# Layer 0's gate sums on TensorE instead of GpSimd and VectorE, in a two-layer graph kernel with a hand-written order

## The chip, the cores and the metric

The kernel runs on one core of one Trainium2 chip. All data are 32-bit floats. The metric is the device time of one execution in microseconds (us), as the median over runs on the chip. The profile shows one execution: TensorE (PE, with its weight loads as PEld), VectorE (DVE), ScalarE (ACT), GpSimd (POOL), SyncE (SP) and the DMA queues.

## The reference

There are 16 batches (graphs) of 1024 nodes with 128 features, and two layers. Layer 0 is a gated graph attention, layer 1 a convolution with four heads; each ends in a residual sum and a layer norm. Cut to what matters:

```python
# layer 0, x: (16, 1024, 128), adj: (16, 1024, 1024) of zeros and ones
h = einsum('bnf,df->bnd', x, Ww) + Wb
e = einsum('bjl,bkl->bjk', einsum('bjd,dl->bjl', h, A), h)
e = e + swapaxes(e, 1, 2)
attention = softmax(where(adj > 0, e, 0.0), axis=1) * adj
h_prime = relu(einsum('bij,bjk->bik', attention, h))
ic = sigmoid(h_prime @ wi_u + x @ wi_x)[..., None]
fc = sigmoid(h_prime @ wf_u + x @ wf_x)[..., None]
oc = sigmoid(h_prime @ wo_u + x @ wo_x)[..., None]
x = layernorm(x + oc * tanh(ic * h_prime + fc * x))

# layer 1, H = 4 heads
h = einsum('bnf,hfd->hbnd', x, conv_w) + conv_b[:, None, None, :]
scores = einsum('hbni,hij,hbmj->hbnm', h, attn_w, h)
hh = relu(einsum('hbnm,hbmd->hbnd', tanh(adj * scores), h))
x = layernorm(x + relu(relu(mean(hh, axis=0)) + x))
```

The change is about the three gates `ic`, `fc`, `oc`, and there about the part `h_prime @ w_u`: per batch 1024 nodes times 128 features against three weight vectors.

## The kernel before

**Batches and layers are interleaved.** Layer 1 of batch b is the backbone: 4 heads of 8 steps, each step two half steps, so 64 half steps a batch. In one step TensorE computes the scores of 128 nodes against all 1024 in two products of 512 columns (`sc`), VectorE multiplies them with the adjacency into `pair`, and ScalarE takes tanh. The pairs of the steps before are multiplied with `h` by a scheme of seven products of 64 x 256 tiles in place of eight (`early`, `late`, in `Pair.product`). It needs sums of rows, which VectorE makes (`differ`, `differ_more`), and one sum that a DMA of GpSimd's queue accumulates.

**Layer 0 of batch b + 1** is strewn over these half steps. Its pieces have letters: W, L, X load; Q and H project; S scores one row block, T turns it over a DRAM transfer; E finds the edges (GpSimd); A takes the row maximum and the exponentials; B weights the row and multiplies it with h (TensorE, G for the second half); R0 and R1 apply relu and leave `hpT`, h_prime with features on partitions (128 x 1024). P turns `hpT` on VectorE and sends it through DRAM to `hp`, with nodes on partitions. Then the gates, I (the inner sum and tanh), O (the outer one), V and N (layer norm), and D, which turns the new x into `x1T` for layer 1.

**The gates before** (batch 1 on). h_prime @ w_u is computed from `hp`: GpSimd multiplies all of `hp` with one broadcast weight vector, `wu_b`, into the buffer of `x1T` (`weigh_hp`, line 620), and VectorE sums over the features (`sum_hp`, lines 626 and 628). This is done three times, once for each gate, one after the other because all three use one buffer: Y multiplies for f, F sums for f and takes its sigmoid, f scales x by that gate on ScalarE and multiplies for i, i sums and multiplies for o, o sums and takes the sigmoid of i and o. The part x @ w_x comes with h's projection: `multiply_h` (line 86 through `mm`) multiplies with 132 columns, of which three are the gates' and are kept in `gate`. Batch 0, whose layer 0 runs ahead of all else, gets its gates from TensorE in `rows_half`, through `ident_g`: the identity with the three u vectors (`gate_u`) beside it.

**The order is written out by hand.** Each engine works in program order, and the program order is in three lists of 64 strings, one string per half step: `FIRST` for batch 0, `PLAN` for the middle ones, `LAST` for batch 15. A plain name is a piece of batch b + 1, `+` marks batch b + 2; `d` and `m` are VectorE's sums for the pairs, `u`, `r` and `j` projections and sums for layer 1, `e` a step of the layer's end. In batch 14 there is no batch 16, so the `+` pieces fall away.

**Products on TensorE.** Once layer 1 has begun, `mm` splits each product into two halves of 64 weight columns, which lie in different column halves of the array. Each half of a 32-bit product appears in the profile as two records, each with a weight load:

```python
for c in range(2):
    nc.tensor.matmul(out[ts(c, HD)], lhsT[:, ts(c, HD)], rhs, start=start, stop=stop)
```

**PSUM.** `small` gives a piece one of three buffers (`ps_sc`), the same that the scores of layer 1 rotate through. A product can start when the engine that reads the buffer's last content is done with it.

Of the kernel before, what the change touches and what calls it, by code (L numbers as in the profile page):

```python
# [11 lines left out]
F32 = mybir.dt.float32  # L12
BF16 = mybir.dt.bfloat16
U8 = mybir.dt.uint8
AF = mybir.ActivationFunctionType
ALU = mybir.AluOpType
AX = mybir.AxisListType
PSUM = bass.MemoryType.PSUM

P = 128  # L20
EPS = 1e-5
# [3 lines left out]
def two_layer_adjacency_kernel(  # L25
# [19 lines left out]
    nc = tc.nc  # L45
    B, N, D = x.shape
    H = conv_w.shape[0]
    assert D == P and N % 512 == 0
    NB = N // P
    NH = N // 512  # L50
    BH = NB // NH

    consts = ctx.enter_context(tc.tile_pool(name="consts", bufs=1))
    adjp = ctx.enter_context(tc.tile_pool(name="adjp", bufs=NB))
    sb = ctx.enter_context(tc.tile_pool(name="sb", bufs=2))
# [7 lines left out]
    def small(name):  # L63

        k = len(made) % (3 + len(spare))
        made.append(name)
        if k < 3:
            return ps_sc.tile([P, 512], F32, tag="sc", name=name)
        n = N if spare[k - 3] == "acc1" else 512
        return ps_acc.tile([P, n], F32, tag=spare[k - 3], name=name)[:, :512]  # L70

# [8 lines left out]
    def mm(out, lhsT, rhs, start, stop):  # L80

        if not begun:
            nc.tensor.matmul(out, lhsT, rhs, start=start, stop=stop)
            return
        for c in range(2):
            nc.tensor.matmul(out[ts(c, HD)], lhsT[:, ts(c, HD)], rhs, start=start, stop=stop)  # L86

    warm = sb.tile([P, N], F32, tag="sum", name="warm", bufs=1)
    nc.vector.memset(warm[:, :P], 0.0)
# [27 lines left out]
    gate_u, gate_x = ident_g[:, D : D + 3], wwT_g[:, D : D + 3]  # L117

    wu_b = consts.tile([P, 3, D], F32, name="wu_b")

    def load_late_weights():
        nc.sync.dma_start(cw_in[0:1], conv_b.rearrange("(o h) d -> o h d", o=1))
        nc.sync.dma_start(cw_last, conv_w[:, D - 1, :].partition_broadcast(P))
        for f0, f1 in ((0, 112), (112, D - 1)):
            nc.sync.dma_start(
                cw_in[1 + f0 : 1 + f1], conv_w[:, f0:f1, :].rearrange("h f d -> f h d")
            )
        nc.sync.dma_start(aw, attn_w.rearrange("h i j -> i h j"))  # L130
        for g, w in enumerate((wi_u, wf_u, wo_u)):
            nc.sync.dma_start(gate_u[:, g : g + 1], w.rearrange("(d o) -> d o", o=1))
            nc.sync.dma_start(wu_b[:, g, :], w.partition_broadcast(P))

# [189 lines left out]
    def turn(dst, src, name):  # L326

        t = sb.tile([P, N], F32, tag="turn", name=f"turn_{name}", bufs=2)
        nc.vector.transpose(t.rearrange("p (k d) -> p k d", d=P), src)
        hop(dst, t, name)  # L330
# [10 lines left out]
    adj_t, x1_t, x1T_t = {}, {}, {}  # L341
# [6 lines left out]
    def layer0(b):  # L348
# [5 lines left out]
        t = {}  # L354
# [257 lines left out]
            hpT = t["hpT"].rearrange("p (k d) -> p k d", d=P)  # L612
            turn(t["hp"], hpT, f"hp_{b}")

        def weigh_hp(g):

            if b not in x1T_t:
                x1T_t[b] = sb.tile([P, N], F32, tag="x1T", name=f"x1T_{b}")
            t["hw"] = x1T_t[b].rearrange("p (k d) -> p k d", d=P)
            nc.gpsimd.tensor_mul(  # L620
                t["hw"], t["hp"], wu_b[:, g : g + 1, :].to_broadcast([P, NB, D])
            )

        def sum_hp(g):
            hw = sb.tile([P, NB, 1], F32, tag="hw", name=f"hws_{b}_{g}")
            nc.vector.tensor_reduce(hw, t["hw"], AX.X, ALU.add)  # L626
            gate = t["gate"][:, :, g : g + 1]
            nc.vector.tensor_add(gate, hw, gate)

        def sigmoid(gate):  # L630

            nc.scalar.activation(gate, gate, AF.Exp, scale=-1.0)
            nc.vector.tensor_scalar_add(gate, gate, 1.0)
            nc.vector.reciprocal(gate, gate)

        def forget():
            t["u"] = sb.tile([P, NB, D], F32, tag="u", name=f"u0_{b}", bufs=1)
            t["x1"] = sb.tile([P, NB, D + 1], F32, tag="x1", name=f"x1_{b}")
            for k in range(NB):
                nc.scalar.mul(t["u"][:, k, :], t["x"][:, k, :], t["gate"][:, k, 1:2])  # L640
            nc.gpsimd.memset(t["x1"][:, :, 0:1], 1.0)

        def gate_f():
            sum_hp(1)
            sigmoid(t["gate"][:, :, 1:2])

        def gate_f_end():
            forget()
            weigh_hp(0)

        def gate_i():
            sum_hp(0)
            weigh_hp(2)

        def gates_io():
            sum_hp(2)
            sigmoid(t["gate"][:, :, 0:3:2])

        def inner(halves):
            u, gate, hp = t["u"], t["gate"], t["hp"]  # L660
# [32 lines left out]
        if b == 0:  # L693
            pieces.update(R2=end_second, q0=copy_q, b0=partial(back, 0))
            for j in (1, 2):
                pieces[f"M{j}"], pieces[f"X{j}"] = partial(mask, j), partial(exponentials, j)
            for q in range(NH):
                for name, piece in (
                    ("R", end_first), ("P", rows_half), ("c", copy_half), ("a", add_gate),
                    ("e", exp_gate), ("d", end_gate), ("f", forget_half),  # L700
                ):
                    pieces[f"{name}{q}"] = partial(piece, q)
                pieces[f"T0.{q}"] = partial(turn_first_score, q)
                pieces[f"S1.{q}"] = partial(score, 1, [q])
        else:
            pieces.update(
                P=turn_hp, Y=partial(weigh_hp, 1), F=gate_f, f=gate_f_end, i=gate_i, o=gates_io,
                R0=partial(end_half, 0), R1=partial(end_half, 1),
            )
            for j in range(NB):  # L710
                pieces[f"G{j}"] = partial(back, j, [1])
            for v in "abcd":
                pieces[f"V{v}"] = lambda: next(t["norm", 0])
# [38 lines left out]
    h1_t, u_t = {}, {}  # L752

    def turn_x1(b):
        turn(x1T_t[b].rearrange("p (k d) -> p k d", d=P), x1_t[b][:, :, 0:D], f"x1_{b}")

    def turn_first_x1(x1, q):
# [309 lines left out]

    ORDER = [m for i in range(BH) for m in (i, i + BH)]
    first, second, join = layer0(0), layer0(1), join_weights()
    run(first, "W L0 L1 L2 L3 L4 L5 L6 L7")  # L1070
    load_late_weights()
# [51 lines left out]
    for g in range(2):  # L1123
# [2 lines left out]


    PLAN = [
        "B3", "E4 L5 T5 m15", "", "j0.0 A4 L6", "", "d0", "E5 T6 m0", "E6 r2 r3 B4",
        "d1 L7 r6 A5 r7", "m1", "B5 j0.1", "A6 d2", "+W E7", "", "u1.0 e", "+Q0 u1.1 m2 B6 A7",  # L1130
        "B7 j1.1 j1.0", "d3", "+L0 m3 e X R0 e", "+E0 G0 G1 G2 e e e G3 G4 G5",
        "G6 G7 e +L1 R1 d4", "P e m4", "", "", "", "+L2", "+E1 d5", "m5 d6 u2.0 e", "+H0 Y +h0",
        "+Q1 m6 F +S0", "+T0", "+H1 u2.1 +A0 +h1 j2.0", "d7 +S1 f i +T1", "", "m7", "o d8 +S2",
        "j2.1", "+S3 u3.0 +T2 m8 I0", "I1", "", "", "d9 O0 +S4", "m9 O1", "Va", "Vb u3.1",
        "+E2 d10", "+S5 m10 Vc", "+T3", "Vd N0 d11 j3.0", "+H2 m11", "+h2 +B0 +L3", "D",
        "d12 +S6", "m12 +T4", "j3.1", "+S7", "d13", "m13 +A1", "", "+E3", "+B1 u0.0",
        "+A2 u0.1 +A3", "+L4", "d14 r5 r0 m14 r4 +B2 d15 r1",
    ]

    FIRST = [  # L1140
        "S5 A0", "m15", "E1 B0", "u1.0", "L3 A1", "S6 d0 E2", "A2 S7 B1 u1.1 m0",
        "L4 B2 T3 T4 L5", "d1 E3", "E4 A3 j1.0 m1", "E5", "T5 B3 d2", "+W A4 L6", "E6", "B4 L7",
        "+Q0 m2 T6 A5", "", "E7 A6 B5 u2.0 d3 u2.1", "+L0 m3 B6 j1.1", "+E0 A7", "+L1 B7 d4",
        "m4", "R0", "", "G0", "+L2 G1 G2", "+E1 G3 G4 d5", "G5 m5 G6 d6 G7", "j2.0 R1 P +H0 +h0",
        "+Q1 m6 +S0 X", "+T0", "+H1 +A0 +h1", "d7 +S1 +T1", "Y", "m7 j2.1", "F d8 +S2", "",
        "+S3 f +T2 m8 i", "", "o", "I0 u3.0 I1", "d9 +S4", "O0 m9 O1", "u3.1", "Va Vb", "+E2 d10",
        "+S5 m10 Vc", "Vd +T3 j3.0", "N0 d11", "+H2 m11", "+h2 +B0 +L3", "D", "d12 +S6",
        "j3.1 m12 +T4", "", "+S7", "d13", "m13 +A1", "", "+E3", "+B1 u0.0", "u0.1 +A2 +A3", "+L4",
        "d14 r0 r5 m14 +B2 d15 r4 r1",
    ]  # L1150

    LAST = [
        "", "m15", "", "j0.0", "", "d0 m0", "", "r7", "r3", "d1", "u1.0 r2 r6 m1", "j0.1 d2", "e",
        "u1.1 j1.1", "m2", "d3", "", "m3", "j1.0", "", "d4", "u2.0 m4", "", "d5", "", "m5 j2.0",
        "", "e", "", "u2.1 d6", "m6", "", "d7", "", "j2.1 m7", "u3.0", "d8", "m8", "", "", "",
        "d9", "m9", "u3.1", "e", "j3.1 d10", "m10", "", "d11 j3.0", "", "m11", "e", "", "e", "e",
        "", "e", "e", "", "e", "", "", "", "",
    ]
    begun.append(True)
    spare.clear()  # L1160
# [2 lines left out]
    for b in range(B):  # L1163
# [37 lines left out]
        for step in range(H * NB):  # L1201
            hd, m = divmod(step, NB)
            i, half = divmod(m, 2)
# [95 lines left out]
```

## Time and profile before

| what | value |
|---|---|
| median of 3 runs | 2328.73 us (2328.29 to 2329.71) |
| the profiled execution | 2329.8 us, its span 2328.0 us |
| layer 1 of batch 0 begins at | 63.4 us |
| one middle batch | 142.5 us |
| batch 15 begins at | 2200.6 us |
| last matmul ends at | 2321.8 us |
| GpSimd's gate products (line 620) | 45, 2.48 us each |
| VectorE's gate sums (line 626) | 45, 1.21 us each |
| gate adds (line 628), scalings (633), reciprocals (634) | 11.5, 8.7, 6.9 us in all |

How to read it: times of rows are sums over the execution, "busy" is the union of an engine's records, and a product's row counts records, four to a product that `mm` splits. The share of an engine is a mean over 16 batches, whose first and last differ from the middle ones; the windows by batch show this. The granted TensorE clock was full but for 3.4 us at half speed, from 163.5 us on.

### The profile page before, as it was taken

How to read it: one execution, taken by the hardware profiler on the slowest of the kernel's cores; microseconds unless marked ns; L12 is line 12 of the kernel's file. 1: busy time of each engine (PE TensorE's matmuls, PEld its weight loads, DVE VectorE, ACT ScalarE, POOL GpSimd, SP SyncE). 2: the span in 40 equal slices, each digit the busy share in tenths (PEclk: the TensorE clock that was granted, in tenths of full speed). 3: DMA queues.
4: the chain of work that ended last, by engine and by line, in shares of the span. 5: the costliest groups of instructions: out<-in, count | busy, mean ns of one | idle time of the engine just before them, and what ended most of it. 6: DMA issues, size and time to landing. Idle time of an engine off the chain costs nothing. (4 is left out here: it accounts for less than half of the span.)

```text
span 2328.0 us, 40444 instructions
## 1 busy us (share of the span) xinstructions
PE 2304.9 (99%) x14693; PEld 1074.7 (46%) x14693; DVE 2039.5 (88%) x3689; ACT 1292.4 (56%) x2186; POOL 1308.2 (56%) x1129
## 2 busy tenths in 40 slices
PE   9999999999999999999999999999999999999998
PEld 5345544444444444444444444444444444444444
DVE  7879898998989889898898988889898898988777
ACT  6545564555556555555555555556556555554444
POOL 2645656556565655656466564665645646555342
PEclk9999999999999999999999999999999999999999
DMA  4647565575655656556565565756647565573421
GB/s 146 164 95 199 124 144 154 114 195 133 170 133 111 190 137 173 132 123 173 134 180 129 129 179 114 184 133 135 171 105 201 130 165 135 106 184 86 123 55 37
DMA packets 498090, 327.27 MB, mean 141 GB/s; under 512 B 391139, under 2 KB 416482, under 8 KB 497891
## 3 DMA queue, kind: packets, MB, share of 16 engines
q1 hardware_dynamic: 459149, 250.68, 38.8%
q0 software_dynamic: 38448, 73.94, 18.1%
q8 instruction: 116, 1.90, 0.3%
q14 instruction: 83, 0.68, 0.1%
q10 hardware_dynamic: 294, 0.07, 0.0%
HBM read 199.04 MB, written 59.51 MB: 111 GB/s over the span
## 5 line engine op out<-in xcount | busy, mean ns | idle before, releaser
L86 PE MATMUL sc<-uT,x1T 128*64 128x512 f32 x4096 | 1054.4, 593 | 4.0 <-ACT uT L283 1.9
L836 ACT ACTIVATE pair<-pair 128x1024 f32<-128x1024 f32 x504 | 533.3, 1058 | 588.9 <-DVE pair L829 278.7
L892 POOL DMA_DIRECT2D pair<-pair x252 | 225.5, 895 | 723.3 <-ACT pair L836 158.2
L831 DVE TENSOR_TENSOR pair<-sc,adj 128x512 f32<-128x512 f32 x504 | 339.1, 682 | 105.1 <-PE sc L86 103.7
L86 PEld LDWEIGHTS sc<-uT,x1T 128*64 128x64 f32 x4096 | 294.1, 137 | 293.8 <-issue 156.8
L829 DVE SCALAR_TENSOR_TENSOR pair<-sc,adj 128x512 f32<-128x512 f32 x504 | 343.0, 684 | 86.0 <-PE sc L86 81.5
L475 POOL TENSOR_SCALAR edge<-ring 128x1024 uint8<-128x1024 f32 x120 | 361.0, 3010 | 25.2 <-DMA ring<-in_adjT_dram 23.4
L840 DVE TENSOR_TENSOR pair<-pair 128x1024 f32<-128x1024 f32 x252 | 328.8, 1305 | 10.6 <-ACT pair L836 10.6
L864 PE MATMUL late<-pair,h 128*64 128x256 f32 x2016 | 304.8, 380 | 3.7 <-DMA pair<-pair 3.6
L864 PE MATMUL early<-pair,h 128*64 128x256 f32 x2016 | 304.1, 379 | 1.3 <-ACT pair L836 1.3
L864 PE MATMUL late<-pair,hx 128*64 128x256 f32 x2016 | 304.1, 380 | 0.0
L864 PEld LDWEIGHTS early<-pair,h 128*64 128x64 f32 x2016 | 145.3, 137 | 289.7 <-issue 255.2
L86 PE MATMUL acc<-R,h 128*64 128x512 f32 x960 | 232.2, 592 | 1.3 <-ACT h L524 1.3
L864 PEld LDWEIGHTS late<-pair,h 128*64 128x64 f32 x2016 | 145.6, 137 | 185.4 <-issue 129.5
L864 PEld LDWEIGHTS late<-pair,hx 128*64 128x64 f32 x2016 | 146.6, 137 | 178.3 <-issue 142.7
L891 DVE TENSOR_TENSOR pair<-pair 128x512 f32<-128x512 f32 x252 | 187.8, 745 | 3.2 <-PE early L864 2.6
L504 ACT ACTIVATE R<-R,nmax 128x1024 f32<-128x1024 f32 x126 | 144.7, 1148 | 62.8 <-DVE nmax L500 56.4
L492 DVE CUSTOM_DVE_ANT_0 R<-R,edge 128x1024 f32<-128x1024 f32 x120 | 172.8, 1440 | 3.3 <-POOL edge L475 3.0
L527 DVE TENSOR_TENSOR R<-R,ring 128x1024 f32<-128x1024 f32 x120 | 161.6, 1347 | 0.0
L864 PE MATMUL early<-pair,hx 128*64 128x256 f32 x1008 | 152.0, 379 | 0.0
L620 POOL TENSOR_TENSOR x1T<-hp,wu_b 128x1024 f32<-128x1024 f32 x45 | 111.7, 2482 | 69.5 <-DVE hws L626 63.3
L936 POOL TENSOR_TENSOR w<-w 128x512 f32<-128x512 f32 x63 | 84.8, 1346 | 96.5 <-DVE w L926 96.3
(214 smaller groups left out, 2831.2 us busy)
## 6 DMA issues: line engine op xcount, KB each, us to landing
adj<-in_adjT_dram SPq DMA_DIRECT2D x128, 512.0 KB, 4.2
pair<-pair POOLq DMA_DIRECT2D x252, 256.0 KB, 3.7
ring<-in_adjT_dram SPq DMA_DIRECT2D x120, 512.0 KB, 5.0
xT<-in_xT_dram SPq DMA_DIRECT2D x16, 512.0 KB, 7.2
x<-in_x_dram SPq DMA_DIRECT2D x16, 512.0 KB, 5.2
dram_hp<-turn_hp SPq DMA_DIRECT2D x15, 512.0 KB, 2.6
hp<-dram_hp SPq DMA_DIRECT2D x60, 128.0 KB, 3.1
dram_x<-turn_x SPq DMA_DIRECT2D x15, 512.0 KB
```

Of the source, the lines that this page charges most:

```text
L86: nc.tensor.matmul(out[ts(c, HD)], lhsT[:, ts(c, HD)], rhs, start=start, stop=stop)
L475: engine.tensor_scalar(m, t["adj", j], 0.0, None, ALU.is_gt)
L492: nc.vector.tensor_tensor_reduce(to[:, ks], s[:, ks], t["edge", j][:, ks], 1.0, nmax, ALU.mult, ALU.max, top)
L504: nc.scalar.activation(row(j), row(j), AF.Exp, bias=t["nmax", j], accum_out=t["z", j])
L527: nc.vector.tensor_mul(s[:, ks], s[:, ks], adj[:, ks])
L829: nc.vector.scalar_tensor_tensor(to, psv, -1.0, adj, op0=ALU.mult, op1=ALU.mult)
L831: nc.vector.tensor_mul(to, psv, adj)
L836: nc.scalar.activation(s, s, AF.Tanh)
L840: nc.vector.tensor_add(t[:, X3 : N12 + 1 : N12 - X3, :], t[:, N12 : N12 + 1, :].to_broadcast([P, 2, 512]), t[:, B22 : B11 + 1, :],)
L864: nc.tensor.matmul(out[ts(q, HD)], w, self.t[:, at, ts(q, HN)], start=(i == 0 and p in (1, 3, 5, 4)), stop=(i == BH - 1), skip_group_check ...
L891: nc.vector.tensor_add(t[:, B22], t[:, B22], t[:, N12])
L892: nc.gpsimd.dma_start(t[:, N21], t[:, B22], accum_op=ALU.add)
```

## The change

From batch 1 on, `h_prime @ w_u` is computed by TensorE from `hpT`, which lies with features on partitions as a product needs it: for each of the 8 blocks of 128 nodes one product with `gate_u` (128 x 3), so the block of `hpT` is the stationary operand and three columns stream. All 24 columns of a batch go into one PSUM tile, `pg`; VectorE adds them to `gate` in one add of 128 x 24, and the sigmoid of all three gates is taken in one chain. `weigh_hp`, `sum_hp`, `wu_b` and its three loads fall away; the x1T buffer is taken when D needs it, no longer for the gates. The piece Y is now the products, the add and the exponential, F the rest of the sigmoid, f the scaling of x; i and o are gone. P and the transfer to `hp` stay, as I needs `hp`.

The three lists are laid out anew. In `PLAN`, R0 moves from half step 18 to 23, R1 from 20 to 27, P from 21 to 28, Y from 28 to 30, F from 29 to 32, f from 32 to 34, I0 from 37 to 35, h0 from 28 to 31, S0 from 29 to 32, T0 from 30 to 33, S3 from 37 to 44 beside S4, and the loads, edges and row pieces of the next batch (L, E, A, B) move by a few half steps each. D stays in 51.

```diff
-    wu_b = consts.tile([P, 3, D], F32, name="wu_b")
...
-            nc.sync.dma_start(wu_b[:, g, :], w.partition_broadcast(P))
...
-        def weigh_hp(g):
-
-            if b not in x1T_t:
-                x1T_t[b] = sb.tile([P, N], F32, tag="x1T", name=f"x1T_{b}")
-            t["hw"] = x1T_t[b].rearrange("p (k d) -> p k d", d=P)
-            nc.gpsimd.tensor_mul(
-                t["hw"], t["hp"], wu_b[:, g : g + 1, :].to_broadcast([P, NB, D])
-            )
-
-        def sum_hp(g):
-            hw = sb.tile([P, NB, 1], F32, tag="hw", name=f"hws_{b}_{g}")
-            nc.vector.tensor_reduce(hw, t["hw"], AX.X, ALU.add)
-            gate = t["gate"][:, :, g : g + 1]
-            nc.vector.tensor_add(gate, hw, gate)
-
-        def sigmoid(gate):
-
+        def gates_T(q):
+
+            if q == 0:
+                t["pg"] = small(f"pg_{b}")[:, : NB * 3]
+            for k in range(q * BH, (q + 1) * BH):
+                mm(
+                    t["pg"][:, ts(k, 3)], t["hpT"][:, ts(k, P)], gate_u,
+                    start=True, stop=True,
+                )
+
+        def gates_in():
+            for q in range(NH):
+                gates_T(q)
+            gate = t["gate"].rearrange("p k g -> p (k g)")
+            nc.vector.tensor_add(gate, t["pg"], gate)
             nc.scalar.activation(gate, gate, AF.Exp, scale=-1.0)
+
+        def gates_end():
+            gate = t["gate"].rearrange("p k g -> p (k g)")
             nc.vector.tensor_scalar_add(gate, gate, 1.0)
             nc.vector.reciprocal(gate, gate)
...
-                P=turn_hp, Y=partial(weigh_hp, 1), F=gate_f, f=gate_f_end, i=gate_i, o=gates_io,
+                P=turn_hp, Y=gates_in, F=gates_end, f=forget,
...
     def turn_x1(b):
+        x1T_t[b] = sb.tile([P, N], F32, tag="x1T", name=f"x1T_{b}")
         turn(x1T_t[b].rearrange("p (k d) -> p k d", d=P), x1_t[b][:, :, 0:D], f"x1_{b}")
...
     PLAN = [
...
-        "G6 G7 e +L1 R1 d4", "P e m4", "", "", "", "+L2", "+E1 d5", "m5 d6 u2.0 e", "+H0 Y +h0",
-        "+Q1 m6 F +S0", "+T0", "+H1 u2.1 +A0 +h1 j2.0", "d7 +S1 f i +T1", "", "m7", "o d8 +S2",
-        "j2.1", "+S3 u3.0 +T2 m8 I0", "I1", "", "", "d9 O0 +S4", "m9 O1", "Va", "Vb u3.1",
...
+        "", "+Q0 +Q1 m3", "A7", "B7", "d4 X", "+L0 +L1", "m4 e R0", "G0 d5 G1 e e G2 j2.0 G3",
+        "e m5", "G4 G5 e", "e G6 G7 R1 d6 +E0", "e P", "+E1 m6 e", "+L2 Y +H0 u2.0", "u2.1 +h0",
+        "F d7 +S0", "+T0 +H1 +h1", "j2.1 f m7", "I0", "I1 +S1 +A0", "+S2 d8 +T1", "m8", "",
+        "d9 u3.0 O0 u3.1", "", "m9 O1", "Va", "+T2 +S3 Vb +T3 +S4", "d10 m10 Vc", "Vd +H2",
...
```

The lists `FIRST` and `LAST` change in the same way.

## The prediction, before the run

> **What bounds the kernel now.** I read the page's busy shares first, then busy time by batch, then what TensorE waits for in the middle batches, then the rows of the work that the change removes, and last the pace of the smallest products.
>
> ```profile
> PE 2304.9 (99%) x14693; PEld 1074.7 (46%) x14693; DVE 2039.5 (88%) x3689; ACT 1292.4 (56%) x2186; POOL 1308.2 (56%) x1129
> ```
>
> TensorE is busy 99% of the span. The share is an average, so the same by batch (columns: window, length, then busy time of PE, weight loads, VectorE, ScalarE, GpSimd). The windows begin at the first layer-1 score product of batches 0, 1, 7, 13, 14 and 15:
>
> ```profile
> 63.40:210.30 146.90, 141.11 (x882) 64.06 (x883) 127.07 (x223) 79.99 (x135) 81.74 (x66) 0.99 0.63 148
> 210.30:352.80 142.50, 142.33 (x924) 71.92 (x922) 127.75 (x229) 80.72 (x136) 84.25 (x71) 1.00 0.61 148
> 1065.70:1208.20 142.50, 142.30 (x924) 65.14 (x922) 128.47 (x229) 80.73 (x136) 84.52 (x72) 1.00 0.61 148
> 1922.00:2064.80 142.80, 142.63 (x922) 65.06 (x920) 129.10 (x230) 80.55 (x136) 84.19 (x71) 1.00 0.61 148
> 2064.80:2200.60 135.80, 130.84 (x826) 58.22 (x824) 113.41 (x203) 67.74 (x114) 71.45 (x66) 1.00 0.46 113
> ```
>
> A middle batch takes 142.5 us and TensorE is idle in 0.2 us of it. A matmul's record runs about 0.166 us past its streaming time (592 ns for 512 columns, against 429 ns from start to start), so shorter gaps are covered. From the starts alone (gaps of over 25 ns beyond the streaming time) I get a lost time of 0.5 to 1.0 us in each of batches 1 to 13, 10.1 us in batch 0, 6.8 us in batch 14, 1.2 us in batch 15 and 7.5 us ahead of 63.4 us. So batches 1 to 13 are pure TensorE work: what is added to TensorE there is added to the time, and what is taken from VectorE and GpSimd is worth only the few gaps that they cause. The largest of these, in batches 1 to 13:
>
> ```profile
> PE sc L86 <- DVE h L411: 3.1, 12, 0.8
> ```
>
> **The change, part by part.** Removed per batch from 1 on: three GpSimd products, three VectorE sums with their adds, one of two sigmoid chains.
>
> ```profile
> L620 POOL TENSOR_TENSOR x1T<-hp,wu_b 128x1024 f32<-128x1024 f32 x45 | 111.7, 2482 | 69.5 <-DVE hws L626 63.3 <-DMA hp<-dram_hp 6.2
> L626 DVE TENSOR_REDUCE hws<-x1T 128x8 f32<-128x1024 f32 x45 | 54.4, 1209 | 0.0
> L628 DVE TENSOR_TENSOR gate<-hws,gate 128x8 f32<-128x8 f32 x45 | 11.5, 257 | 1.6
> ```
>
> That is 111.7 us of GpSimd and 54.4 + 11.5 = 65.9 us of VectorE, less 15 new adds of 128x24 from PSUM at about 0.25 us (3.8 us); half of the small scalings and reciprocals (8.7 + 6.9 us) go too. VectorE loses about 70 us, 4.7 us a batch. By itself this is worth nothing: VectorE works beside a TensorE that has no slack.
>
> *Added: 120 products of 3 columns on TensorE.* Each is split into two column halves, and each half has two records (the 448 records of the 132-column projection are 112 products), so a batch gets 32 loads and 32 matmuls, in 16 rounds of two halves. No row of 64-column weights has so few columns, so I bound it. The nearest row with 64-column weights is the projection, three products of 132 columns:
>
> ```profile
> 988.51 0.84 PE L86 MATMUL pR_h<-wwT_g,xT 128*64 128x132 f32 x12
> 989.18 1.03 PE L86 MATMUL sc<-uT,x1T 128*64 128x512 f32 x4
> ```
>
> From start to start 0.67 us for 6 rounds, 112 ns each: as 512 columns take 429 ns, 132 stream in about 110 ns, so the loads are hidden and cost at most this. That is the upper end: 16 x 112 = 1.8 us a batch, 27 us in all. With 3 columns there is nothing to hide a load behind, and the load sets the pace. The nearest row for that is a product of one column with 128-column weights:
>
> ```profile
> 10.43 0.30 PEld L191 LDWEIGHTS p_bsb<-sb_col,first_w 128*128 128x128 f32 x2
> 10.65 0.19 PEld L83 LDWEIGHTS sc<-xT,qT 128*128 128x128 f32 x1
> 988.08 0.14 PEld L864 LDWEIGHTS early<-pair,h 128*64 128x64 f32 x2 [0.29 <-issue]
> ```
>
> Two loads of 128 columns, then the next: 0.22 us, 0.11 us each. A load of 64 columns is shorter by the streaming of 64 (137 ns against 190), so about 58 ns with the 5 ns that the wide load has above 107. The last line shows the two halves' loads side by side, 0.14 us for both, as long as one. If they overlap in full, a round takes 58 ns: 16 x 58 = 0.93 us a batch, 14 us in all. With one or two semaphore waits ahead of the group (some 50 ns each in the starts) I take 1.0 us, **+15 us**. Below: the rounds can't be faster than their loads, 13 us.
>
> Here the Trainium skill speaks against the change. "TensorE: Matmul & The Clock Gate", Part 3 (The mechanism), says that a load overlaps matmuls in flight only if its row group differs; here all use all 128 rows. Then each round would pay its load (53 ns by that page's columns / 1.2) and on top its matmul, at least the 25 ns that its table of issue gaps gives for up to 64 columns: 16 x 78 = 1.25 us, 19 us in all. The row above disagrees: at 112 ns a round with 110 ns of streaming there is no room for a load that isn't overlapped. The 25 ns alone, without loads, would give 32 x 25 = 0.8 us, 12 us. I stay with the row, 15 us, inside 12 to 27.
>
> *Moved, and given back.* (a) The gap on h. VectorE's max over a score row (L492, 1.44 us in the mean) takes 2.45 us here, while GpSimd multiplies the gates (853.40 to 855.77 us):
>
> ```profile
> 854.40 2.45 DVE L492 CUSTOM_DVE_ANT_0 R<-R,edge 128x1024 f32<-128x1024 f32 x1
> 856.97 0.56 DVE L411 TENSOR_TENSOR h<-pR_h,wb_row 128x396 f32<-128x396 f32 x1
> ```
>
> h comes late, and the score product behind it starts 0.34 to 0.38 us late in each batch. In the new order A0 no longer stands there, h0 has half step 31 to itself and S0 comes in 32: the gap goes, 13 x 0.37 = **-4.8 us**. (b) In batch 14, where no next layer 0 fills TensorE, gaps of 0.68, 0.90, 0.33 and 1.29 us (2136.1 to 2149.1) stand right behind the gates' sums and slowed VectorE work (a 128x512 sum of 1.99 us instead of 0.75). I take two thirds back: **-2 us**. (c) New waits. The gate product takes one of the three PSUM buffers that the scores rotate through, until VectorE has added it; behind its add stand only one mask product (0.68 us) and h0, while TensorE has a projection and a u product (1.5 us) before the buffer comes round: nothing. But S3 and S4 now stand in one half step (44): three score buffers that ScalarE must empty at 0.63 us each, with a tanh of 1.06 us perhaps ahead. TensorE streams 1.9 us in that time; I take 0.15 us a batch, **+2 us**, bounded by 0 and 0.5 a batch (7 us). (d) Batch 0 is laid out anew as well; its 10.1 us of gaps lie mostly ahead of the gates (77 to 112 us); 0, with 4 us either way. (e) GpSimd's queue: the pairs' accumulating DMAs and the hx sums stood behind the gate products, but TensorE shows no wait over the record's tail for them in batches 1 to 13: 0. (f) SyncE loses three loads of the u weights at the start, in the shadow of the first adjacency loads: 0. The transfer of hp keeps its seven half steps (28 to 35, before 21 to 28), some 15 us; the hpT buffer is held until the gate products (30), ahead of T0 (33): 0.
>
> Sum: +15 - 4.8 - 2 + 2 = **+10.2 us**. The profiled execution took 2329.8 us (span 2328.0 and 1.8 around it), 1.1 above the median of 2328.73; a difference carries over, so 2328.7 + 10.2, about 2339.0 us.
>
> **The rivals.**
> 1. *Loads in series.* If the halves' loads don't overlap when nothing streams between, a round is 112 ns or more: 27 + 1 us for the products, 28 - 4.8 = +23, about 2352. For it: a wide load and two half loads carry the same data. Against: two half loads take 0.14 us together. "TensorEngine Tiling (Array Packing)", Key Properties, says that tiles can load and multiply in parallel; this case shows it only beneath a stream.
> 2. *The gain matches the cost.* The new order saves also half of batch 0's gaps (5 us), the rest of batch 14's by half (2 us), and adds no wait at S3: 15 - 4.8 - 2 - 7 = +1, about 2330.
> 3. *Faster.* One mechanism: VectorE's backlog, 4.7 us a batch shorter and no longer slowed by GpSimd, was behind nearly all gaps of batches 0 to 14, some 25 us. If all but 4 us go, 21 us are saved against 13 of products at their floor: -8, about 2321. It decides from 20 us saved on. Against: most of batch 0's gaps lie before any gate work, and 3.4 us at half clock are among them.
>
> **How the numbers follow.** The measurement tells no less than about 0.2% from no change, 4.7 us: slower means above 2333.4. The likeliest case, +15 with its bounds (+4.7 to +15), has 0.60; loads in series 0.20; gain matches cost 0.14; faster 0.06. So slower 0.80, same 0.14, faster 0.06. The range runs from 2331.5, inside the second rival, to 2354, inside the first; about 0.1 is left out on each side.
>
> **What would show it.** Right: a gate group of 32 records per batch, next product 0.9 to 1.1 us after its first; periods of middle batches of 143.0 to 143.5 instead of 142.5; VectorE near 84%, GpSimd near 51%, and no faster for it; no S0 gap. Loads in series: 1.8 us per group and periods over 144. Wrong: middle batches at or under 142.5, which would mean that the group costs under 0.5 us, or batches 0 and 14 shorter by over 10 us together.

## The result, and the profile after

The changed kernel takes 2324.52 us (median of 20 runs), the kernel before 2329.17 us in as many: a ratio of 0.998, 95% interval 0.9973 to 0.9987. It is faster by 4.65 us, where 10 us slower was forecast. On another chip, run once more beside the last experiments, the ratio was 0.9976 (0.9968 to 0.9983). The profiled execution's span is 2322.3 us, 5.7 us under that of before.

The page's first row, to be set against that of before:

```profile
PE 2309.4 (99%) x15173; PEld 1138.2 (49%) x15173; DVE 1946.2 (84%) x3584; ACT 1288.6 (55%) x2171; POOL 1182.6 (51%) x1084
```

TensorE has 480 records more (15 batches of 32) and 4.5 us more of busy time, VectorE 93 us less, GpSimd 126 us less (more than the work that was taken away, as some passes that stay got shorter: VectorE's 120 row maxima went from 172.8 to 150.8 us in all); and the span is shorter although TensorE has more to do. Where, the windows by batch tell (columns as before: window, length, busy time of PE, weight loads, VectorE, ScalarE, GpSimd); they begin at the first score product of batches 0, 1, 7, 13, 14 and 15:

```profile
63.30:203.00 139.70, 138.38 (x909) 70.60 (x910) 120.72 (x212) 77.31 (x129) 71.93 (x63) 1.00 0.66 155
203.00:345.90 142.90, 142.90 (x954) 78.66 (x952) 121.39 (x222) 80.35 (x136) 76.98 (x69) 1.00 0.61 149
1060.80:1203.70 142.90, 142.90 (x954) 66.34 (x952) 121.97 (x222) 80.36 (x136) 75.07 (x68) 1.00 0.62 148
1919.40:2062.30 142.90, 142.90 (x954) 66.37 (x952) 121.09 (x222) 80.43 (x136) 76.36 (x69) 1.00 0.60 148
2062.30:2195.10 132.80, 130.89 (x862) 59.96 (x860) 109.32 (x200) 69.61 (x119) 65.20 (x63) 1.00 0.48 117
```

Batch 0 took 146.9 us and takes 139.7: -7.2. Batches 1 to 13 took 1854.5 us together and take 1859.3: +4.8, some 0.4 each. Batch 14 took 135.8 and takes 132.8: -3.0. The ends (ahead of batch 0, and batch 15 with the tail) give -0.3. The sum is -5.7.

The gate products themselves, in the timeline of TensorE in batch 5:

```profile
843.37 0.61 PE L847 MATMUL late<-pair,hx 128*64 128x256 f32 x4
843.80 1.05 PE L86 MATMUL pg<-ident_g,hpT 128*64 128x3 f32 x32
844.70 0.88 PE L86 MATMUL pR_h<-wwT_g,xT 128*64 128x132 f32 x12
```

From 843.80 to 844.70 is 0.90 us for 16 rounds; from one round's start to the next the records show 58 ns, the price that the prediction took from the loads. So the added term was right, and the answer lies in what the rest of the change gave back.

### The profile page after: what moved, and what is told of

It is laid out like the page before. It is cut to its first block, busy times and chain, and to the rows that moved or that the text cites. A ratio compares the mean times of both kernels' runs of the same rounds, so it can differ in the third digit from the quotient of the medians.

```text
span 2322.3 us, 41249 instructions
## 1 busy us (share of the span) xinstructions
PE 2309.4 (99%) x15173; PEld 1138.2 (49%) x15173; DVE 1946.2 (84%) x3584; ACT 1288.6 (55%) x2171; POOL 1182.6 (51%) x1084
## 4 chain that ended last, share of the span: by engine, by line
PE 96%; DVE 1%; POOL 1%; ACT 1%; issue 1%; DMA 0%; POOLq 0%; ACTq 0%; DVEq 0%
PE sc L86 41%; PE late L847 18%; PE early L847 14%; PE acc L86 9%; PE pT_u L86 4%; PE pR L86 4%; PE pR_h L86 1%; PE pT_q L86 1%; PE pg L86 1%; PE sc L83 1%; POOL edge L472 0%; DMA pair<-pair 0%; PE pR L83 0%; PE acc L83 0%; PE acc_other L83 0%
## 5 line engine op out<-in xcount | busy, mean ns | idle before, releaser
L86 PEld LDWEIGHTS sc<-uT,x1T 128*64 128x64 f32 x4096 | 308.7, 137 | 288.0 <-issue 162.5
L472 POOL TENSOR_SCALAR edge<-ring 128x1024 uint8<-128x1024 f32 x120 | 353.6, 2953 | 100.6 <-DMA ring<-in_adjT_dram 90.2
L823 DVE TENSOR_TENSOR pair<-pair 128x1024 f32<-128x1024 f32 x252 | 338.9, 1345 | 20.2 <-ACT pair L819 20.2
L847 PEld LDWEIGHTS early<-pair,h 128*64 128x64 f32 x2016 | 153.1, 137 | 279.2 <-issue 249.4
L847 PEld LDWEIGHTS late<-pair,h 128*64 128x64 f32 x2016 | 153.2, 137 | 173.8 <-issue 132.2
L847 PEld LDWEIGHTS late<-pair,hx 128*64 128x64 f32 x2016 | 153.3, 137 | 170.9 <-issue 138.5
L874 DVE TENSOR_TENSOR pair<-pair 128x512 f32<-128x512 f32 x252 | 179.3, 711 | 5.8 <-PE early L847 2.6
L524 DVE TENSOR_TENSOR R<-R,ring 128x1024 f32<-128x1024 f32 x120 | 158.4, 1320 | 0.0
L489 DVE CUSTOM_DVE_ANT_0 R<-R,edge 128x1024 f32<-128x1024 f32 x120 | 150.8, 1257 | 0.7 <-POOL edge L472 0.7
L429 ACT ACTIVATE R<-sc,h 128x512 f32<-128x512 f32 (+1 forms) x192 | 107.2, 576 | 49.3 <-PE sc L86 44.7
L86 PE MATMUL pT_u<-x1T,ms 128*64 128x512 f32 x504 | 128.1, 592 | 0.0
```

The costliest lines, as they stand in the source:

```text
L472: engine.tensor_scalar(m, t["adj", j], 0.0, None, ALU.is_gt)
L489: nc.vector.tensor_tensor_reduce(to[:, ks], s[:, ks], t["edge", j][:, ks], 1.0, nmax, ALU.mult, ALU.max, top)
L524: nc.vector.tensor_mul(s[:, ks], s[:, ks], adj[:, ks])
L823: nc.vector.tensor_add(t[:, X3 : N12 + 1 : N12 - X3, :], t[:, N12 : N12 + 1, :].to_broadcast([P, 2, 512]), t[:, B22 : B11 + 1, :],)
L847: nc.tensor.matmul(out[ts(q, HD)], w, self.t[:, at, ts(q, HN)], start=(i == 0 and p in (1, 3, 5, 4)), stop=(i == BH - 1), skip_group_check ...
L874: nc.vector.tensor_add(t[:, B22], t[:, B22], t[:, N12])
```

## The experiments

Each was run in five rounds beside the kernel before on the same chip; ratios are to that kernel. The chips differ a little (before: 2332.01, 2329.79 and 2330.09 us for the first four, the next four and the last two), so ratios are compared, or the spans and batch lengths of the profiled executions.

| run | median us | ratio (95%) | span us | batch 0 | middle batch | batch 14 |
|---|---|---|---|---|---|---|
| before | 2329.17 | 1 | 2328.0 | 146.8 | 142.5 | 135.8 |
| changed | 2324.52 | 0.998 | 2322.3 | 139.7 | 142.9 | 132.8 |
| new gates, old order | 2332.03 | 1.0001 (0.9993 to 1.0009) | 2330.2 | 145.3 | 142.9 | 133.7 |
| new order, no products | 2312.16 | 0.9916 (0.9902 to 0.9929) | 2310.6 | 139.2 | 142.0 | 133.1 |
| old order, no gate sums | 2320.47 | 0.9954 (0.994 to 0.9967) | 2317.7 | 145.2 | 142.0 | 133.7 |
| products unsplit | 2344.49 | 1.0052 (1.004 to 1.0065) | 2340.7 | 141.2 | 144.0 | 135.1 |
| before, h1 ahead of A0 | 2322.93 | 0.997 (0.9957 to 0.9982) | 2322.3 | 145.3 | 142.0 | 137.2 |
| changed, old list of batch 0 | 2330.15 | 1.0002 (0.9994 to 1.001) | 2328.1 | 144.8 | 142.9 | 132.6 |
| GpSimd gates, mended order | 2320.56 | 0.9958 (0.9946 to 0.9971) | 2319.4 | 142.4 | 142.0 | 138.5 |
| the same, batch 15's gates on TensorE | 2315.84 | 0.994 (0.9927 to 0.9952) | 2314.0 | 143.2 | 142.0 | 132.4 |
| the same, batch 1's too | 2316.36 | 0.9948 (0.9934 to 0.9961) | 2313.6 | 139.6 | 142.0 | 133.0 |
| changed, once more | 2324.38 | 0.9976 (0.9968 to 0.9983) | 2321.9 | 139.9 | 142.9 | 132.6 |

The middle batch is the length that most of batches 1 to 13 show. Four of these profiled executions hold a stretch of 3.4 us at half the TensorE clock, which costs some 1.7 us: in batch 0 before the change, with h1 ahead of A0 and with batch 15's gates on TensorE, and in batch 14 with GpSimd's gates in the mended order. Where a reading rests on these batches, the text takes it off.

**New gates, old order.** The gates of the change with the three old lists:

```diff
     PLAN = [
-        "E4 L5", "m15 A3", "", "A4 B3 j0.0", "u1.0", "d0", "m0", "r6 E5 d1 L6 u1.1 T6", "r2",
+        "B3", "E4 L5 T5 m15", "", "j0.0 A4 L6", "", "d0", "E5 T6 m0", "E6 r2 r3 B4",
...
     FIRST = [
-        "S5 A0 E1 u1.0", "T3 m15 B0", "L3 S6", "A1 E2", "", "d0 S7", "m0", "B1 u1.1 A2 d1", "L4",
+        "S5 A0", "m15", "E1 B0", "u1.0", "L3 A1", "S6 d0 E2", "A2 S7 B1 u1.1 m0",
...
     LAST = [
-        "", "m15", "", "d0 j0.0", "", "", "m0", "r3 d1", "r7", "m1", "r6 r2 j0.1", "", "",
+        "", "m15", "", "j0.0", "", "d0 m0", "", "r7", "r3", "d1", "u1.0 r2 r6 m1", "j0.1 d2", "e",
...
```

> The new gates with the three old lists (Y, F, f in their old half steps, i and o empty). Theory A, the new order: what was gained in batch 0 came from its list, so the gaps at 77 to 112 us (4.4 us) are there again; middle batches take 143.0 us as after the change (products +0.9, the gap behind A0 gone), batch 14 is some 3 us shorter than before. Batch 0 near 144 to 146 us, in all 2330 to 2334 us, 1 to 5 us above before. Theory B, the relief of VectorE and GpSimd: the order is worth nothing, batch 0 takes 140 us, in all 2324 to 2326 us as after the change.

The time is that of before, and batch 0 takes 145.3 us. Theory A holds: without the new order the new gates gain nothing in all. These are TensorE's waits from 63 to 125 us, first before, then after the change:

```profile
PE late L864 <- DMA pair<-pair: 2.4, 3, 1.2
PE acc L86 <- ACT h L524: 1.3, 1, 1.3
```

```profile
PE acc L86 <- DVE R L524: 0.6, 1, 0.6
PE sc L86 <- ACT R L429: 0.5, 1, 0.5
PE sc L86 <- ACT uT L280: 0.2, 1, 0.2
```

In the run with the old order, the wait for h, which I should have read, is there again, at the same place as before the change. First TensorE in the kernel before, then in this run:

```profile
75.42 1.03 PE L86 MATMUL sc<-uT,x1T 128*64 128x512 f32 x4
77.71 1.08 PE L86 MATMUL acc<-R,h 128*64 128x512 f32 x4 [1.26 <-ACT h L524]
```

```profile
75.56 1.03 PE L86 MATMUL sc<-uT,x1T 128*64 128x512 f32 x4
77.84 1.08 PE L86 MATMUL acc<-R,h 128*64 128x512 f32 x4 [1.26 <-ACT h L521]
```

And why it is there, in ScalarE's timeline of the kernel before:

```profile
75.87 1.15 ACT L504 ACTIVATE R<-R,nmax 128x1024 f32<-128x1024 f32 x1 [1.11 <-issue]
76.92 0.19 ACT L504 ACTIVATION_READ_ACCUMULATOR R<-R,nmax 128x1 f32 x1
77.02 0.35 ACT L432 ACTIVATE R<-sc,h 128x128 f32<-128x128 f32 x1
77.27 0.39 ACT L524 ACTIVATE h<-h,rz 128x128 f32<-128x128 f32 x1
```

The scaling of h (L524), which TensorE's product waits for, stands behind the exponentials of the next row (L504) and a score copy (L432), since the old half step 6 reads `"A2 S7 B1 u1.1 m0"`: A2 ahead of B1. The new list has `"B1 u1.1 A2 d1"`. In the changed kernel the same product starts without a gap behind the one ahead of it (which piece of the new list ended the waits for the DMA was not followed):

```profile
79.28 0.60 PE L847 MATMUL early<-pair,hx 128*64 128x256 f32 x4
79.71 1.03 PE L86 MATMUL acc<-R,h 128*64 128x512 f32 x4
```

**New order, no products.**

```diff
-            for q in range(NH):
-                gates_T(q)
             gate = t["gate"].rearrange("p k g -> p (k g)")
-            nc.vector.tensor_add(gate, t["pg"], gate)
             nc.scalar.activation(gate, gate, AF.Exp, scale=-1.0)
```

> The changed kernel without the 3-column products and their add: the gates are taken from the part x @ w_x alone. The difference to the changed kernel is the price of the products. If a group costs what its rounds take in the trace (0.9 us), 15 of them are 13.5 us: 2311 us, middle batches at 142.0. Rival: with the products gone another engine bounds (VectorE at 84%), so that only part comes back: 2316 us or more, with new gaps ahead of score products.

A middle batch falls from 142.94 to 142.00 us, the span by 11.7 us. This is TensorE's work with no gap of over 25 ns in most batches, so no other engine bounds it. The products cost 0.94 us in a batch where TensorE is full; in batches 0 and 14, which have gaps anyway, the two runs differ by +0.5 and -0.3 us, so there they cost little or nothing that this pair of executions can tell. Between the two runs in the old order (the one above and the one below) the products are worth 12.5 us of span: the same within 1 us, so products and order add up.

**Old order, no gate sums.**

```diff
         def weigh_hp(g):
...
-            nc.gpsimd.tensor_mul(
-                t["hw"], t["hp"], wu_b[:, g : g + 1, :].to_broadcast([P, NB, D])
-            )
...
         def sum_hp(g):
-            hw = sb.tile([P, NB, 1], F32, tag="hw", name=f"hws_{b}_{g}")
-            nc.vector.tensor_reduce(hw, t["hw"], AX.X, ALU.add)
-            gate = t["gate"][:, :, g : g + 1]
-            nc.vector.tensor_add(gate, hw, gate)
+            return
```

> The kernel before, in its old order, without GpSimd's gate products and VectorE's sums and adds: the gates are taken from the part x @ w_x alone. This is the relief by itself. Theory A (order): the gap behind A0 goes in 13 batches (-4.8 us), batch 14 loses some 3 us of gaps, batch 0 keeps those at 77 to 112 us: 2317 to 2321 us, middle batches at 142.1. Theory B (relief): batch 0 falls to 140 us as well, 2312 to 2314 us.

The relief alone is worth 10.3 us of span (ratio 0.9954), within what theory A allowed. The middle batches are at 142.0, batch 14 at 133.7, and batch 0 stays at 145.2, with its early waits as they were:

```profile
PE late L857 <- DMA pair<-pair: 2.5, 3, 1.2
PE acc L86 <- ACT h L524: 1.3, 1, 1.3
```

Of batch 0's 10.1 us of gaps only 1.7 go here, and that is the stretch at half clock, which this execution doesn't have. So the 5.6 us by which batch 0 is shorter in the changed kernel than with the new gates in the old order come with the new order: both of these kernels have the relief.

The spans of these runs, one step at a time, split the change: -10.3 us for the relief in the old order, +12.5 us for the products (2317.7 to 2330.2) and -7.9 us for the new order (2330.2 to 2322.3), -5.7 us in all. The shares of relief and order hold for this sequence only, as both remove the gap on h in the middle batches.

**Changed, old list of batch 0.** Only `FIRST` is set back, and T5 of batch 2 is added to `PLAN`'s half step 1, where the old list leaves it:

```diff
     PLAN = [
-        "E4 L5", "m15 A3", "", "A4 B3 j0.0", "u1.0", "d0", "m0", "r6 E5 d1 L6 u1.1 T6", "r2",
+        "E4 L5", "m15 T5 A3", "", "A4 B3 j0.0", "u1.0", "d0", "m0", "r6 E5 d1 L6 u1.1 T6", "r2",
...
     FIRST = [
-        "S5 A0 E1 u1.0", "T3 m15 B0", "L3 S6", "A1 E2", "", "d0 S7", "m0", "B1 u1.1 A2 d1", "L4",
+        "S5 A0", "m15", "E1 B0", "u1.0", "L3 A1", "S6 d0 E2", "A2 S7 B1 u1.1 m0",
...
```

> The changed kernel with the list of batch 0 (FIRST) as before, and T5 of batch 2 in PLAN's half step 1, where the old list leaves it. If batch 0's gain is in this list alone, batch 0 takes 145.3 us (as in the run of the new gates in the old order) and the rest is as in the changed kernel: +5.6 us, 2330 us. If it came from the three lists together, or from the gates, batch 0 stays under 142 us and the time at 2325 us.

Batch 0 takes 144.8 us and the span is 5.8 us longer than the changed kernel's, the rest unchanged. That is the whole gain of the change and a little more: with the old list for one batch of sixteen, the change is worth nothing (1.0002).

**Before, h1 ahead of A0.** One half step of `PLAN` in the kernel before; gates as before:

```diff
     PLAN = [
...
-        "+Q1 m6 F +S0", "+T0", "+H1 u2.1 +A0 +h1 j2.0", "d7 +S1 f i +T1", "", "m7", "o d8 +S2",
+        "+Q1 m6 F +S0", "+T0", "+H1 u2.1 +h1 +A0 j2.0", "d7 +S1 f i +T1", "", "m7", "o d8 +S2",
...
```

> The kernel before with one half step of PLAN changed: VectorE's add of h (h1) stands ahead of the row maximum A0 instead of behind it; gates and all else as before. If the gap ahead of the second score block came from h waiting behind an A0 that GpSimd's product slows, 0.37 us goes in 12 to 13 batches: 4.5 us under the kernel before, middle batches at 142.1. Rival: VectorE then waits for TensorE's projection and A0 is later, so that the gap only moves: no change, 142.5.

The middle batches fall to 142.0 us, as far as with all gate sums left out. The swap of two names is worth 5.7 us of span and 7 us by the ratio, more than the change that it is cut out of, and what TensorE waits for in batches 1 to 13 no longer has a row of h:

```profile
PE late L864 <- DMA pair<-pair: 0.9, 1, 0.9
PE early L864 <- ACT pair L836: 0.3, 1, 0.3
```

VectorE indeed waits for the projection now, as the rival said, in its timeline of this run:

```profile
850.65 0.69 DVE L829 SCALAR_TENSOR_TENSOR pair<-sc,adj 128x512 f32<-128x512 f32 x1
852.19 0.57 DVE L411 TENSOR_TENSOR h<-pR_h,wb_row 128x396 f32<-128x396 f32 x1 [0.84 <-PE pR_h L86]
852.67 1.22 DVE L492 CUSTOM_DVE_ANT_0 R<-R,edge 128x1024 f32<-128x1024 f32 x1
```

But its 0.84 us cost nothing: VectorE has that room, TensorE has not. A0 also no longer meets GpSimd's product, which is over at 852.64 us, and takes 1.22 us instead of 2.45:

```profile
850.26 2.38 POOL L620 TENSOR_TENSOR x1T<-hp,wu_b 128x1024 f32<-128x1024 f32 x1
```

**Products unsplit.** In the changed kernel, `mm` with its two halves is left out for the gates:

```diff
-                mm(
+                nc.tensor.matmul(
                     t["pg"][:, ts(k, 3)], t["hpT"][:, ts(k, P)], gate_u,
                     start=True, stop=True,
                 )
```

> The changed kernel with each 3-column product in one piece of 128 weight columns instead of two halves of 64: the same 16 records a batch in 16 loads of 128 columns. If the halves' loads overlap, the whole ones take twice as long: 16 x 112 ns = 1.8 us a batch, +0.9 us each, middle batches at 143.8, about +13 us: 2338 us. If loads are in series whatever their width, the group takes as long as with halves, 0.9 us, and the time is that of the changed kernel, 2324.5 us. A cost of going from halves to whole columns and back would show as a gap ahead of and behind the group.

A middle batch is 1.09 us longer than in the changed kernel, where overlapping loads let 0.9 be expected, and the time is 12.5 us above the kernel before (ratio 1.0052). The span is 18.4 us above the changed kernel's, where 13 was expected: 14.9 us of it in batches 1 to 13, the rest in batches 0 and 14. In TensorE's timeline:

```profile
848.91 0.60 PE L847 MATMUL late<-pair,hx 128*64 128x256 f32 x4
849.44 1.95 PE L617 MATMUL pg<-ident_g,hpT 128*128 128x3 f32 x16
851.32 0.90 PE L86 MATMUL pR_h<-wwT_g,xT 128*64 128x132 f32 x12
```

The 16 records follow at 112 ns each, 1.79 us; two halves side by side need 58 ns. So the halves' loads do overlap, and the rival of loads in series is out. The rest, some 0.2 us, is at the two ends: the product ahead has streamed by 849.34 and the group begins at 849.44, and behind the last record (851.13) the next begins 0.18 us later, not 0.11. The Trainium skill, "TensorEngine Tiling (Array Packing)", Key Properties, says that a change of tiling mode drains TensorE. A loss of about 0.1 us at each end fits that, but the run can't tell a drain from a load that nothing hides.

**GpSimd gates, mended order.** The gates of before, h1 ahead of A0 in both lists, and half steps 0 to 27 of `FIRST` from the changed kernel:

```diff
     PLAN = [
...
-        "+Q1 m6 F +S0", "+T0", "+H1 u2.1 +A0 +h1 j2.0", "d7 +S1 f i +T1", "", "m7", "o d8 +S2",
+        "+Q1 m6 F +S0", "+T0", "+H1 u2.1 +h1 +A0 j2.0", "d7 +S1 f i +T1", "", "m7", "o d8 +S2",
...
     FIRST = [
-        "S5 A0", "m15", "E1 B0", "u1.0", "L3 A1", "S6 d0 E2", "A2 S7 B1 u1.1 m0",
+        "S5 A0 E1 u1.0", "T3 m15 B0", "L3 S6", "A1 E2", "", "d0 S7", "m0", "B1 u1.1 A2 d1", "L4",
...
-        "j2.0 R1 P +H0 +h0", "+Q1 m6 +S0 X", "+T0", "+H1 +A0 +h1", "d7 +S1 +T1", "Y", "m7 j2.1",
+        "R1 P +H0 +h0 j2.0", "+E1 m6 +L2 +S0", "+T0", "+H1 +h1 +A0", "d7 +S1 +T1", "Y", "m7 j2.1",
...
```

> The gates on GpSimd and VectorE as before; h1 ahead of A0 in PLAN and FIRST; and FIRST's half steps 0 to 27 taken from the changed kernel, its gate chain from 28 on as before. If order and gates are separate matters, both gains of the order come without the products' price: -4.5 us in the middle batches and -4 to -6 us in batch 0, some 9 to 11 us under the kernel before and about 5 us under the changed one. If the new order only works with the relief of VectorE, batch 0 stays over 144 us and the time within 5 us of before.

Batch 0 falls by 3 us against the run with h1 alone (145.3 to 142.4), with VectorE and GpSimd as loaded as before. But 1.7 us of these are the stretch at half clock, which that run has in batch 0 and this one has not: the new half steps give some 1.3 us here, or 2.8 against the kernel before, where 4 to 6 were expected and the whole list gave 5.6 with the new gates. (These are single executions: before and with h1 ahead of A0, batch 0 runs the same list, and took 146.8 and 145.3 us.) The waits from 77 to 112 us are gone; one of 1.5 and one of 1.3 us at 157 to 160 us stay, behind the gate sums and I0 and I1 in one half step:

```profile
157.42 1.08 PE L86 MATMUL sc<-xT,qT 128*64 128x512 f32 x4 [1.33 <-DVE pair L831]
159.67 1.08 PE L86 MATMUL sc<-uT,x1T 128*64 128x512 f32 x4 [1.17 <-ACT uT L283]
```

By ratio it is some 5 us faster than the changed kernel (0.9958 against 0.998): the gap on h is gone, and there are no products to pay for. Its batch 14 is 2.7 us longer than before, 1.7 us of it by a stretch at half clock at its end and 1.0 by a longer wait for a DMA.

**Batch 15's gates on TensorE, then batch 1's too.** Both begin from that run; the second has `b in (1, B - 1)` in the first line, the changed kernel's whole `FIRST`, and A3 and S7 in `PLAN`'s half steps 0 and 2:

```diff
+            if b == B - 1:
+                pieces.update(Y=gates_in, F=gates_end, f=forget)
+                del pieces["i"], pieces["o"]
```

> As the run with GpSimd's gates in the mended order, but batch 15's gates, which are computed during batch 14, where TensorE has room, come from the 3-column products. Batch 14 falls from 135.8 to about 133.5 us: 2 us under that run. If batch 14's gaps have nothing to do with the gates' sums, it costs the products' 0.9 us and gains nothing.

Batch 14 falls by 6.0 us to 132.4 (1.7 of them the half clock of the run that it is set against) and the time to 2315.84 us, 0.994 of before: faster than both kernels. Here TensorE waits for VectorE anyway, and taking the sums off VectorE is worth more than the 0.9 us.

> As the run with batch 15's gates alone on TensorE, and batch 1's gates, computed during batch 0, from TensorE too, with the changed kernel's whole list FIRST (its gate chain is shorter, so I and O come earlier and apart); A3 and S7 of batch 2 are taken up in PLAN's half steps 0 and 2. If the gap of 1.5 and 1.3 us at 157 to 160 us is that of GpSimd's longer gate chain and of I0 and I1 in one half step, batch 0 falls from 143.2 to about 140 us against 0.9 us of products already in it: some 3 us under that run. If it comes from somewhere else, batch 0 stays at 143 and the time rises by up to 1 us.

Batch 0 falls to 139.6 us as expected. Of the 3.6 us, 1.7 are again the half clock of the run that it is set against; against the run with GpSimd's gates, which has none in batch 0, it is 2.8. The gates and the later half steps of `FIRST` changed together, so what is owed to which is not shown. But batch 1, which has to take up A3 and S7 in the old `PLAN`, rises to 143.9 (+1.9). The span is 0.4 us shorter, the time is the same within the runs' spread.

> The changed kernel as it is, beside the others on the same chip, so that they can be set against it: 0.998 of the kernel before, 4 to 6 us less, with batch 0 at 140, middle batches at 142.9 and batch 14 at 132.8 us.

That is what it showed: 0.9976, with the batches as in the table.

## Why the prediction was wrong, point by point

- **TensorE bounds the kernel:** right. In the changed kernel TensorE's busy share fills the middle batches to the last tenth, and 70 us less of VectorE's work and 112 us of GpSimd's were worth only the gaps they caused: 10.3 us in the old order, 1.7 of it by the half clock.
- **The products, +15 us:** right in size, a little high. 58 ns a round, 0.90 us a group, 13.5 us in 15 groups by the trace, 12 us by the runs without them, as two batches had room for them. The 19 us worked out from the Trainium skill's rule on row groups ("TensorE: Matmul & The Clock Gate", The mechanism) are too high: 0.90 us a group was measured, not 1.25. What speaks against the rule is the projection, whose rounds of 112 ns with 110 ns of streaming leave no room for a load of their own. The 58 ns don't decide it, since a load of 53 ns, the estimate by that page's columns / 1.2, with 3 columns behind it would fit into them. And the rule was cited short: the same section lets a load go ahead into the background weight buffer too.
- **(a) The gap on h, -4.8 us:** right in place on the clock, wrong in name and too small. It is h1 and the second score block (384 columns), not h0 and S0. The middle batches had 8.5 us of gaps in all; without the products' rounds 1.3 us are left: -7.2 us. The run with h1 ahead of A0 shows that no relief was needed for it, the one without gate sums that the relief does it as well: either brings the middle batches to 142.0.
- **(b) Batch 14, -2 us:** right in kind, too small. Its gaps fall from 6.8 us to 2.6 besides the products, -4.2.
- **(c) New waits at S3 and S4, +2 us:** wrong. No middle batch shows a wait there.
- **(d) Batch 0, 0 with 4 us either way:** this is the step that failed. Its gaps fall from 10.1 us to 2.3 besides the products: -7.8 us, where nothing was put down. I saw that most of them lay ahead of any gate work, and took that as a reason why the change would not touch them, although the same change laid out anew the very half steps in which they lay. The waits were in the trace with their names: h scaled behind the next row's exponentials, pairs waiting for a DMA of GpSimd's queue. Reading the new list at the first of these places would have shown B1 ahead of A2. With the new gates in place, the list `FIRST` is worth 5.1 to 5.6 us of batch 0 (the runs with the old list and with the old order). The remaining 2 us or so are mostly the half clock. With the old gates, the list's first 28 half steps gave only 1.3 to 2.8 us, so part of the gain seems to need list and gates together; that was not taken apart.
- **The sum:** +13.5 - 7.2 - 4.2 - 7.8 = -5.7 us, the span's difference to within the small terms left out (the ends, a few more streamed columns). The forecast was +10.2. Of the 15.9 us between them, (d) is 7.8, (a) 2.4, (b) 2.2, (c) 2.0 and the products 1.5: all erred the same way. With (d) right and the rest as forecast, the sum would have been +2.4.
- **The rivals.** The second, gain matches cost, had named these terms: a gain in batch 0's order, the rest of batch 14, no wait at S3. It put the savings at 14 us, and they were 19. The third, faster, had VectorE's backlog behind nearly all of the gaps; of 19 us saved, some 10 came with the relief in the old order and some 8 with the new order. The result, 4.65 us under the kernel before, lies on the line between the two. Of the signs that were named, the group of 0.90 us and the 142.9 us of a middle batch spoke for the prediction, the 10.2 us by which batches 0 and 14 together got shorter against it.
- About 1.7 us of batch 0's gap in the profiled execution of before are the 3.4 us at half clock, which came behind the gaps at 160 to 163 us. The new gates alone shorten these gaps (in the old order one of 0.43 us is left there), so the change takes the occasion away; but whether the clock falls differs by execution, as the last section shows.

## What to carry to other kernels

When a change comes with a new order, cost the order by itself: list the gaps of the bounding engine by place, read which instruction ended each wait and what stood ahead of it on its engine, and look these up in the new order. On the engine that is full, look for work that can stand elsewhere; here the gates on GpSimd cost nothing in the middle batches once two names were swapped, and TensorE took them at a clear profit in batch 14, where it had room. A gain that comes with a change need not come from its main idea: with batch 0's old order the same gates were worth nothing. And before two single executions are compared, look at their clocks: here a stretch at half clock made up 1.7 of the 3.0 and of the 3.6 us by which batch 0 got shorter from one run to the next.

## What the runs showed of the hardware

- A product of 3 columns takes its time from the columns of its weights: two halves of 64 columns side by side every 58 ns, whole 128 columns every 112 ns, and about 0.1 us at each change between the two forms.
- Two VectorE passes that read two tensors in SBUF took longer beside a GpSimd product of 128x1024: the row maximum 2.45 us against 1.22 without, a 128x512 sum 1.99 us against 0.7. Not every pass did: the mask product of 128x512 at 850.65 us above, whose scores come from PSUM, took its usual 0.69 us in the middle of such a product.
- Each of the four stretches at half clock that came before the last matmul began a whole number of windows of 3.413 us after the first clock record of its execution (46, 46, 45 and 639 windows). By the starts of its products, TensorE was idle for 2.1, 2.2, 2.1 and 2.4 us of the window just ahead of them. In the twelve executions, no other window was idle for over 2.0 us but one of 2.1 (h1 ahead of A0, in batch 14), which the full clock followed. In the mended order the two gaps of 1.50 and 1.34 us, 2.8 together, fell into two windows, and the clock stayed full. The idle time within one window thus sorts these executions, but for the one case on the edge, and where the gaps lie against the windows differs by execution. No run was made to test this, or to find the limit.
